# Second expert layer: token lists in place of cleared, scattered rows

## The chip, the cores and the metric

The kernel runs on one core of one Trainium2 chip. The metric is the device time of one launch in microseconds (us). A core has a matrix engine (TensorE, in the profile PE, with its weight loads as PEld), a vector engine (VectorE, DVE), an activation engine (ScalarE, ACT), a general engine (GpSimd, POOL) and a queue engine (SyncE, SP). They run side by side and wait for each other by semaphores. DMAs are issued by SP, ACT or POOL (queue entries are shown as SPq, ACTq, POOLq); one with row numbers in on-chip memory (gather, scatter, scatter-add) is issued by POOL and is shown as DMA_INDIRECT.

## The reference

Two transformer layers on x [4, 512, 256] (2048 tokens), each a cross attention on a context [4, 1601, 256] and a mixture-of-experts layer, all in fp32:

```python
x = x + xattn0(ctx, layernorm(x))      # 8 heads of 128; keys: 1601 context rows and 512 latents
x = x + moe0(layernorm(x))             # 8 experts, top 2, a capacity for each expert
x = x + xattn1(ctx, layernorm(x))      # 8 heads of 32, no bias
x = x + moe1(layernorm(x))             # 8 experts, top 2 by threshold, no capacity

def moe1(x):
    logits = x @ Wr + br
    thresh = second largest logit of each token
    weights = softmax(where(logits >= thresh, logits, -inf))
    h = gelu(x @ W1[e] + b1[e])                       # every expert e, 256 -> 1024
    return sum over e of weights[:, e] * (h @ W2[e] + b2[e])
```

Only two experts of a token have a weight, so the kernel sorts tokens by expert and computes tiles of 256 tokens of one expert.

## The kernel before, in words

The kernel has four stages, one after another on PE.

*First attention* (lines 528 to 898). A loop has 128 steps: 4 batches, 8 heads, 4 row tiles of 128. A step computes scores (L735, ten matmuls), their maximum (L743, DVE, `top`), the softmax (L749, ACT, into one of two `attn` buffers), then `exchange`: sixteen DMAs (L756) that swap 32-row blocks into `swapped`, twelve on SP's queue and four on ACT's. `turn` (L764, DVE) makes of it the transposed probabilities `pT`, which `weigh` (L772, PE) multiplies by the values a step or two later. Keys, values and the LayerNorm of the next batch's context (`ctx_b`) are spread over the steps as small pieces. Ahead of the loop, on SP, `clear_rows` (L370 to 380) fills two tables in HBM with empty rows, and `clear_slots` (POOL's queue) clears those of the first expert layer.

*First expert layer*, then *second attention*. During the second attention `route2` of the batch before runs in steps between other work: it normalises the rows of x (`pay`), finds each token's two experts, its weights and its place in the order of its expert, writes x with its weighted second bias to `out` (plain store), and scatters the rows (L521, POOL) into `rows_a` (2048 rows of 265 numbers: 256 of each expert, tokens of batches 0 to 2) or `rows_b` (18,688 rows: a place for every token and expert, all tokens). A row carries the normalised x, the token's number as a float, and its eight weights. Each of these scatters waits for the one before, since they write the same tensor. The framework orders instructions within each engine by what it knows of their readiness, so an engine's order isn't the order of the program text; the second attention has an order written out.

*Second expert layer* (lines 1375 to 1690). First 8 tiles, one for each expert, with the first 256 rows of `rows_a`; they need nothing of the last batch, whose routing runs between them (`routing`). Then 13 tiles (`SURE`) whose expert and first place come from a table worked out on the chip; further ones stand under a condition. In iteration k the loop does `hidden` of tile k (L1445, L1453), fetches tile k+2 (rows, and the expert's weights `w_e`, 2052 KB), makes tile k+1 `ready` (`turned`: transposes and a copy, L1433 and L1434; `told`: the token numbers `to`, L1395, and the weights `share`, L1423, L1594, L1595), and then `results` of tile k-1 (`second`, L1464; scaling into `y`, L1491; scatter-add into `out`, L1477, POOL). Rows have three buffers, `w_e` four, `to`, `share` and `y` five. Rows of the first 8 tiles come by plain SP loads, the later ones by POOL gathers (L1571; weights by L1583).

Of the kernel before, what the change touches and what calls it, by code (L numbers as in the profile page):

```python
# [8 lines left out]
F32 = mybir.dt.float32  # L9
I32 = mybir.dt.int32  # L10
# [6 lines left out]
P = 128  # L17
# [31 lines left out]

T = B * S  # L50
# [3 lines left out]
ROWS = E * PLACES  # L54
NG = (2 * T - 2 * G + E * (G - 1)) // G
SURE = 13
PAY = D + 1 + E
# [10 lines left out]
def xattn_ffn_twice(ctx: ExitStack, tc: tile.TileContext, a: dict, out: bass.AP):  # L68
# [107 lines left out]
    rows_a = dram.tile([E * G, PAY], F32, name="rows_a")  # L176
    rows_b = dram.tile([ROWS + G, PAY], F32, name="rows_b")
# [177 lines left out]
    taken_a = const.tile([P, E], F32, name="taken_a")  # L355

# [13 lines left out]
    def clear_rows(empty):  # L370

        nc.gpsimd.memset(empty, 0.0)
        nc.gpsimd.memset(empty[:, :, D : D + 1], NOWHERE)
        for rows in (rows_a, rows_b):
            n = rows.shape[0]
            for i in range(0, n, 4 * P):
                some = rows[i : min(i + 4 * P, n), :]
                nc.sync.dma_start(
                    some.rearrange("(p r) d -> p r d", p=P), empty[:, : some.shape[0] // P, :]
                )  # L380

    def route2(b, two, psum, tag, first=0, n=NT):
# [8 lines left out]
        for t in range(n):  # L391
            nc.vector.tensor_scalar(
                pay[:, t, :D],
                xb[:, t, :],
                mv[:, t, 0:1],
                rs[:, t : t + 1],
                ALU.subtract,
                ALU.mult,
            )
            nc.vector.tensor_scalar(  # L400
                pay[:, t, D : D + 1], lane, float((b * NT + first + t) * P), None, ALU.add
            )
# [39 lines left out]
        nc.vector.tensor_copy(pay[:, :, D + 1 :], wb)  # L442
# [74 lines left out]
        for rows, at in ((rows_a, place_a), (rows_b, place_b))[b == B - 1 :]:  # L517
            for k in range(2):
                for t in range(n):
                    j = b * NT + first + t  # L520
                    nc.gpsimd.indirect_dma_start(  # L521
                        out=rows[:, :],
                        out_offset=bass.IndirectOffsetOnAxis(ap=at[k][:, j : j + 1], axis=0),
                        in_=pay[:, t, :],
                        in_offset=None,
                        bounds_check=E * G - 1 if rows is rows_a else ROWS - 1,
                        oob_is_err=False,
                    )
                    yield


    with ExitStack() as st:
# [280 lines left out]
        empty = one.tile([P, 4, PAY], F32, tag="lat", name="empty")  # L813
        clear_rows(empty)
        clear_slots(empty[:, :, :D])
# [562 lines left out]
    with ExitStack() as st:  # L1378
# [8 lines left out]

        spare = st.enter_context(tc.tile_pool(name="d_spare", bufs=1))

        def told(rows, share_of):  # L1390

            to = five.tile([P, GR], I32, tag="to", name="to")
            share = five.tile([P, GR], F32, tag="share", name="share")
            for r in range(GR):
                nc.vector.tensor_copy(to[:, r : r + 1], rows[r][:, D : D + 1])  # L1395
                share_of(share[:, r : r + 1], rows[r][:, D + 1 :])
            return rows, to, share
# [4 lines left out]
        def first_tile(e):  # L1402

            rows = []
            for r in range(GR):
                got = three.tile([P, PAY], F32, tag=f"rows{r}", name=f"rows{r}")
                nc.sync.dma_start(got, rows_a[e * G + r * P : e * G + (r + 1) * P, :])
                rows.append(got)
            if e == 0:
                w2 = one.tile([P, WIDE - WB1], F32, name="w2_first")  # L1410
                nc.sync.dma_start(w2, a["wall"][:P, WB1:])
                w = lambda i, n: (
                    first_weights[i // D][:, i % D : i % D + n]
                    if i < WB1
                    else w2[:, i - WB1 : i - WB1 + n]
                )
            else:
                t = four.tile([P, WIDE], F32, tag="w", name="w_e")
                nc.sync.dma_start(t, a["wall"][e * P : (e + 1) * P, :])
                w = columns(t)  # L1420

            def share_of(to, weights):
                nc.vector.tensor_copy(to, weights[:, e : e + 1])  # L1423

            return w, rows, share_of
# [140 lines left out]
        def further_tile(i, three=three, four=four):  # L1566

            rows = []
            for r in range(GR):
                got = three.tile([P, PAY], F32, tag=f"rows{r}", name=f"rows{r}")  # L1570
                nc.gpsimd.indirect_dma_start(  # L1571
                    out=got,
                    out_offset=None,
                    in_=rows_b[:, :],
                    in_offset=bass.IndirectOffsetOnAxis(
                        ap=state["x_idx"][:, r, i : i + 1], axis=0
                    ),
                    bounds_check=ROWS + G - 1,
                    oob_is_err=False,
                )  # L1580
                rows.append(got)
            t = four.tile([P, WIDE], F32, tag="w", name="w_e")
            nc.gpsimd.indirect_dma_start(  # L1583
                out=t,
                out_offset=None,
                in_=a["wall"],
                in_offset=bass.IndirectOffsetOnAxis(ap=state["w_idx"][:, i : i + 1], axis=0),
                bounds_check=E * P - 1,
                oob_is_err=False,
            )  # L1590

            def share_of(to, weights):
                of = two.tile([P, E], F32, tag="told", name="told")
                nc.vector.tensor_tensor(of, weights, state["mine"][:, i, :], ALU.mult)  # L1594
                nc.vector.tensor_reduce(to, of, AX.X, ALU.add)  # L1595

            return columns(t), rows, share_of

# [5 lines left out]

        rest = routing()
        fetched = [first_tile(0), first_tile(1)]
        more = [lambda e=e: first_tile(e) for e in range(2, E)]
        more += [lambda i=i: further_tile(i) for i in range(SURE)]
        more.append(lambda: further_tile(SURE, spare, spare))

        def ready(w, rows, share_of):
            return (w, turned(rows), *told(rows, share_of)[1:])

        last = None
        next(rest)
        here = ready(*fetched.pop(0))
        for i in range(E + SURE):
            w, xT, to, share = here
            hT = hidden(w, xT)
            for _ in range(2):  # L1620
                next(rest, None)
            if more:
                fetched.append(more.pop(0)())
            if i + 1 < E + SURE:
                here = ready(*fetched.pop(0))
            next(rest, None)
            if last:
                results(*last)
            next(rest, None)
            last = (w, to, share, hT, T - S if i < E else T)  # L1630
# [4 lines left out]
        n_tiles = nc.values_load(state["counts"][0:1, 0:1], min_val=0, max_val=NG)  # L1635
        ties = nc.values_load(state["counts"][0:1, 1:2], min_val=0, max_val=E * T)

        def beyond(i, fetched=None):
            with tc.If(n_tiles > i):
                w, xT, to, share = ready(*(fetched or further_tile(i)))  # L1640
                results(w, to, share, hidden(w, xT))
                if i + 1 < NG:
                    beyond(i + 1)

        beyond(SURE, fetched.pop())
# [3 lines left out]
        with tc.If(ties > 0):  # L1649
            for b in range(B):  # L1650
                for t0 in range(0, NT, GR):
                    rows, acc = [], spare.tile([P, GR, D], F32, tag="acc", name="acc")
                    nc.vector.memset(acc, 0.0)
                    for r in range(GR):
                        j = b * NT + t0 + r
                        got = spare.tile([P, PAY], F32, tag=f"rows{r}", name=f"again{r}")
                        nc.vector.memset(got, 0.0)
                        for of, at in ((rows_a, place_a), (rows_b, place_b)):
                            nc.gpsimd.indirect_dma_start(
                                out=got,  # L1660
                                out_offset=None,
                                in_=of[:, :],
                                in_offset=bass.IndirectOffsetOnAxis(
                                    ap=at[0][:, j : j + 1], axis=0
                                ),
                                bounds_check=of.shape[0] - 1,
                                oob_is_err=False,
                            )
                        rows.append(got)
# [16 lines left out]
                    for r in range(GR):  # L1686
                        to = spare.tile([P, 1], I32, tag="to", name="to_t")
                        nc.vector.tensor_copy(to, rows[r][:, D : D + 1])
                        add_out(acc[:, r, :], to)
# [66 lines left out]
```

## Time and profile before

| | |
|---|---|
| Runs | 3011.76 to 3015.57 us, median 3014.13 (3 runs) |
| Profiled execution | 3014.63 us, its span 3012.6 us, mean granted PE clock 0.965 |
| PE busy | 2781.7 us (92% of the span), weight loads 1846.2 |
| DVE, ACT, POOL busy | 1444.5, 931.1, 473.7 us |
| Moved by DMA | 295.95 MB, mean 98 GB/s |
| Row scatters L521 | 24 into rows_a (32.1 us of POOL), 32 into rows_b (38.5) |
| Scatter-adds L1477 | 42, 66.4 us of POOL |

In a line of the timeline the columns are start, duration, engine, line, operation, output and inputs with shapes, count, and in brackets the idle time ahead and what ended it. A line of waits says which engine waited at which line for what: total us, times, longest. The page cuts the span into 40 equal slices; a digit is the busy share in tenths.

### The profile page before, as it was taken

What the parts mean: (1) busy time and instruction counts of PE and PEld (TensorE: products, weight loads), DVE (VectorE), ACT (ScalarE), POOL (GpSimd) and SP (SyncE); (2) the same over time, 40 slices, a digit from 0 to 9 for tenths busy, and PEclk for the clock granted to TensorE, in tenths of its full rate; (3) what the DMA queues carried; (4) which work ended last, traced back from release to release, by engine and by line L of the source; (5) the groups of instructions that cost most, each with busy time, mean ns of one, the idle gap of its engine ahead of it and who ended that gap; (6) DMA issues with size and microseconds to landing.
All of it is one profiled execution on the core that took longest, in us unless ns stands there. A gap on an engine that the chain in (4) does not pass through costs nothing. (4 is left out here: it accounts for less than half of the span.)

```text
span 3012.6 us, 35574 instructions
## 1 busy us (share of the span) xinstructions
PE 2781.7 (92%) x13426; PEld 1846.2 (61%) x13426; DVE 1444.5 (48%) x2324; ACT 931.1 (31%) x1312; POOL 473.7 (16%) x340
## 2 busy tenths in 40 slices
PE   5699999999999999999997999788988888898998
PEld 2466676666666667666665566544444444467887
DVE  4256447554476444464444100177775757751110
ACT  2233234232343333332321212123433434341221
POOL 1000000100001000010000100122424434343442
PEclk9899999999999999999998999889999999999999
DMA  8743334433343333333334233210101110045652
GB/s 297 234 123 94 99 92 105 112 96 92 94 113 104 98 86 95 93 102 97 92 96 148 93 98 105 66 27 14 30 26 36 30 35 22 13 172 165 193 171 73
DMA packets 165103, 295.95 MB, mean 98 GB/s; under 512 B 43287, under 2 KB 81752, under 8 KB 161848
## 3 DMA queue, kind: packets, MB, share of 16 engines
q1 hardware_dynamic: 124024, 204.45, 24.2%
q0 software_dynamic: 16320, 53.42, 5.9%
q10 hardware_dynamic: 24576, 35.68, 4.6%
q8 instruction: 109, 1.79, 0.3%
q14 instruction: 74, 0.61, 0.1%
HBM read 97.86 MB, written 49.76 MB: 49 GB/s over the span
## 5 line engine op out<-in xcount | busy, mean ns | idle before, releaser
L743 DVE TENSOR_REDUCE top<-ps_s 128x1 f32<-128x2113 f32 x128 | 301.8, 2358 | 578.9 <-PE ps_s L735 578.9
L772 PE MATMUL ps_o<-pT,v 128*128 128x256 f32 x2176 | 520.9, 381 | 7.8 <-DVE pT L764 7.8
L735 PE MATMUL ps_s<-kT,qT 128*128 128x512 f32 (+1 forms) x1280 | 489.0, 527 | 26.7 <-ACT attn L749 26.3
L772 PEld LDWEIGHTS ps_o<-pT,v 128*128 128x128 f32 x2176 | 410.9, 191 | 124.8 <-issue 69.9
L735 PEld LDWEIGHTS ps_s<-kT,qT 128*128 128x128 f32 x1280 | 241.5, 191 | 276.3 <-issue 239.9
L749 ACT ACTIVATE attn<-ps_s,top 128x2113 f32<-128x2113 f32 x128 | 258.9, 2023 | 486.1 <-DVE top L743 411.5
L764 DVE STREAM_TRANSPOSE pT<-swapped 128x2176 f32<-128x2176 f32 x128 | 312.4, 2441 | 70.2 <-DMA swapped<-attn 59.4
L1141 DVE TENSOR_REDUCE tops<-ps_s 128x2 f32<-128x800 f32 (+1 forms) x256 | 241.0, 984 | 150.7 <-PE ps_s L1133 150.6
L1180 PE MATMUL ps_w<-asked,keyed 64*128 64x256 f32 (+1 forms) x1664 | 243.7, 418 | 45.7 <-DVE tops L1141 39.4
L685 PE MATMUL ps_k<-kvin,wkv 128*128 128x512 f32 (+1 forms) x640 | 261.9, 533 | 5.2 <-ACT kT L692 5.2
L718 PE MATMUL ps_v<-wkv,kvin 128*128 128x256 f32 x1088 | 253.5, 381 | 0.0
L1202 POOL TENSOR_TENSOR sum<-sum,pT 128x1024 f32<-128x1024 f32 x80 | 197.0, 2463 | 334.4 <-ACT pT L1193 243.5
L1180 PEld LDWEIGHTS ps_w<-asked,keyed 64*128 64x128 f32 (+1 forms) x1664 | 150.4, 193 | 155.6 <-DVE tops L1141 79.7
L1193 ACT ACTIVATE pT<-ps_w 128x1024 f32<-128x1024 f32 (+1 forms) x176 | 178.2, 1023 | 195.4 <-PE ps_w L1180 191.8
L718 PEld LDWEIGHTS ps_v<-wkv,kvin 128*128 128x128 f32 x1088 | 204.9, 190 | 32.7 <-issue 3.4
L692 ACT ACTIVATE kT<-ps_k,bqk 128x512 f32<-128x512 f32 (+1 forms) x160 | 97.1, 620 | 268.1 <-DMA swapped<-attn 128.8
L685 PEld LDWEIGHTS ps_k<-kvin,wkv 128*128 128x128 f32 x640 | 116.5, 192 | 81.0 <-issue 67.1
L1202 DVE TENSOR_TENSOR sum<-sum,pT 128x1024 f32<-128x1024 f32 x96 | 153.3, 1597 | 6.2 <-ACT pT L1193 3.0
L725 ACT COPY v<-ps_v 128x512 f32<-128x512 f32 x144 | 79.8, 560 | 226.2 <-PE ps_v L718 154.0
L1445 PE MATMUL ps_h<-xT,w_e 128*128 128x256 f32 x640 | 143.7, 383 | 3.7 <-issue 3.7
L1133 PE MATMUL ps_s<-kT,qT 32*128 32x400 f32 (+1 forms) x1024 | 142.1, 582 | 3.2 <-ACT pT L1193 2.6
L1464 PE MATMUL ps_y<-w_e,hT 128*128 128x256 f32 x640 | 144.4, 385 | 0.0
(261 smaller groups left out, 2635.6 us busy)
## 6 DMA issues: line engine op xcount, KB each, us to landing
swapped<-attn SPq DMA_DIRECT2D x1536, 68.0 KB
swapped<-attn ACTq DMA_DIRECT2D x512, 68.0 KB
rows_b<-empty SPq DMA_DIRECT2D x36, 530.0 KB
w<-in_w_dram SPq DMA_DIRECT2D x16, 1024.0 KB
w_e<-in_wall_dram SPq DMA_DIRECT2D x7, 2052.0 KB
cT<-in_ctxT_dram SPq DMA_DIRECT2D x4, 1601.0 KB
keyed<-kT SPq DMA_DIRECT2D x32, 200.1 KB
ctx_b<-in_ctx_dram SPq DMA_DIRECT2D x4, 1536.0 KB
```

The source lines that it names most:

```text
L685: nc.tensor.matmul(ps[:, :n], lhsT=wkv[:, c, hs], rhs=flat_kvin[c][:, j0 : j0 + n], start=c == 0, stop=c == DC - 1,)
L718: nc.tensor.matmul(ps[:, k, :], lhsT=flat_kvin[c][:, j * P : (j + 1) * P], rhs=wkv[:, c, cols], start=c == 0, stop=c == DC - 1,)
L735: nc.tensor.matmul(flat[:, j0 : j0 + n], lhsT=qT[:, t * P : (t + 1) * P], rhs=kT[:, j0 : j0 + n], start=True, stop=True,)
L743: nc.vector.tensor_reduce(top, flat[:, :L], AX.X, ALU.max, negate=True)
L749: nc.scalar.activation(attn[:, :L], flat[:, :L], AF.Exp, bias=top, accum_out=total)
L764: nc.vector.transpose(pT[:, :, k * P : (k + 1) * P].rearrange("p c (a i) -> p a c i", a=4), swapped.rearrange("p a (c i) -> p a c i", i=32),)
L772: nc.tensor.matmul(ps, lhsT=v[:, j - parts[part][0], (h % 2) * DH0 : (h % 2 + 1) * DH0], rhs=pT[:, j, :], start=j == 0, stop=j == NB - 1,)
L1141: nc.vector.tensor_reduce(tops[u][:, t, 2 * pair : 2 * pair + 2, k], pss[pair][:, :, : hi - lo], AX.X, ALU.max,)
L1180: nc.tensor.matmul(ps[:r, s, pair * QH : (pair + 1) * QH], lhsT=keyed[o][64 * s : 64 * s + 64, pair, j * P : j * P + r], rhs=asked[u % 3][ ...
L1193: nc.scalar.activation(pT[:r], ps[:r], AF.Exp)
L1202: (nc.gpsimd if k else nc.vector).tensor_tensor(to, to, pT[:r], ALU.add)
L1464: nc.tensor.matmul(ps, lhsT=hT[:, f, r * P : (r + 1) * P], rhs=w(WB1 + f * D, D), start=f == 0, stop=f == FC - 1,)
```

## The change

The rows of the second expert layer are no longer scattered by expert. Each batch's `pay` (256 + 8 numbers a row, the token number gone) is stored in token order by a plain SP DMA into `rows_a` (1537 rows) and `rows_b` (2049 rows; both for batches 0 to 2), the last row being zeros. What is scattered by expert and place is the token's number alone, 4 bytes, into `list_a` (2048) and `list_b` (18,688), which are filled with a number that stands for no token by one small DMA each. A tile loads its list one tile ahead of its rows (`listed`: an SP load for the first 8 tiles, two POOL gathers for later ones), and gathers its rows by it (`fetched`: two POOL gathers, for the first 8 tiles too). The list is also the address of the scatter-adds (`to`, now in seven buffers), so the casts of L1395 and the lane addition in `route2` fall away. The branch for ties reads rows in order; it isn't entered here.

```diff
-PAY = D + 1 + E
+PAY = D + E
...
-    rows_a = dram.tile([E * G, PAY], F32, name="rows_a")
-    rows_b = dram.tile([ROWS + G, PAY], F32, name="rows_b")
+    list_a = dram.tile([E * G, 1], I32, name="list_a")
+    list_b = dram.tile([LIST + G, 1], I32, name="list_b")
+    rows_a = dram.tile([TA + 1, PAY], F32, name="rows_a")
+    rows_b = dram.tile([T + 1, PAY], F32, name="rows_b")
...
-        for rows in (rows_a, rows_b):
-            n = rows.shape[0]
-            for i in range(0, n, 4 * P):
-                some = rows[i : min(i + 4 * P, n), :]
-                nc.sync.dma_start(
-                    some.rearrange("(p r) d -> p r d", p=P), empty[:, : some.shape[0] // P, :]
-                )
+    def clear_lists(zeros, nobody):
+        for rows, of, n in ((rows_a, list_a, TA), (rows_b, list_b, T)):
+            per = of.shape[0] // P
+            nc.gpsimd.memset(nobody[:, :per], n)
+            nc.sync.dma_start(of.rearrange("(p r) o -> p (r o)", p=P), nobody[:, :per])
+            nc.sync.dma_start(rows[n : n + 1, :], zeros)
...
-            nc.vector.tensor_scalar(
-                pay[:, t, D : D + 1], lane, float((b * NT + first + t) * P), None, ALU.add
-            )
...
+            nc.sync.dma_start(
+                rows[at0 : at0 + n * P, :].rearrange("(t p) d -> p t d", p=P), pay
+            )
             for k in range(2):
                 for t in range(n):
                     j = b * NT + first + t
                     nc.gpsimd.indirect_dma_start(
-                        out=rows[:, :],
+                        out=of[:, :],
                         out_offset=bass.IndirectOffsetOnAxis(ap=at[k][:, j : j + 1], axis=0),
-                        in_=pay[:, t, :],
+                        in_=token[:, j : j + 1],
...
+        seven = st.enter_context(tc.tile_pool(name="d_seven", bufs=7))
...
-                nc.vector.tensor_copy(to[:, r : r + 1], rows[r][:, D : D + 1])
...
+        def listed(k, pool):
+            to = pool.tile([P, GR], I32, tag="to", name="to")
+            if k < E:
+                of = list_a[k * G : (k + 1) * G, :].rearrange("(p r) o -> p (r o)", p=P)
+                nc.sync.dma_start(to, of)
+                return to
+            for r in range(GR):
+                nc.gpsimd.indirect_dma_start(
+                    out=to[:, r : r + 1],
+                    out_offset=None,
+                    in_=list_b[:, :],
+                    in_offset=bass.IndirectOffsetOnAxis(
+                        ap=state["x_idx"][:, r, k - E : k - E + 1], axis=0
+                    ),
...
+        def fetched(k, to, three=three, four=four):
+            of, n = (rows_a, TA) if k < E else (rows_b, T)
             rows = []
             for r in range(GR):
                 got = three.tile([P, PAY], F32, tag=f"rows{r}", name=f"rows{r}")
-                nc.sync.dma_start(got, rows_a[e * G + r * P : e * G + (r + 1) * P, :])
+                nc.gpsimd.indirect_dma_start(
+                    out=got,
+                    out_offset=None,
+                    in_=of[:, :],
+                    in_offset=bass.IndirectOffsetOnAxis(ap=to[:, r : r + 1], axis=0),
...
+        lists = [listed(k, seven) for k in range(3)]
+        tiles = [fetched(k, lists[k]) for k in range(2)]
...
-            if more:
-                fetched.append(more.pop(0)())
+            if k + 2 <= n_tiles:
+                pools = (three, four) if k + 2 < n_tiles else (spare, spare)
+                tiles.append(fetched(k + 2, lists[k + 2], *pools))
+            if k + 3 <= n_tiles:
+                lists.append(listed(k + 3, seven if k + 3 < n_tiles else spare))
```

## The prediction

> **What bounds the kernel now.** I read first the forty slices of the page, to find where TensorE (PE) is not the bound:
>
> ```profile
> PE   5699999999999999999997999788988888898998
> PEclk9899999999999999999998999889999999999999
> DMA  8743334433343333333334233210101110045652
> ...
> rows_b<-empty SPq DMA_DIRECT2D x36, 530.0 KB
> ```
>
> A slice is 75.3 us. PE is at 90% or more nearly everywhere; only the first two slices fall short while DMA is at its fullest, and the clearing of `rows_b` stands there. The table by stretch (columns: PE, its weight loads, DVE, ACT, POOL; clock, DMA share, GB/s) and PE's waits from 45 to 150 us show it closer:
>
> ```profile
> 40.00:100.00 60.00, 52.26 (x168) 30.26 (x167) 11.03 (x13) 19.03 (x30) 5.18 (x8) 0.94 1.02 380
> 100.00:110.00 10.00, 0.00 (x0) 0.00 (x0) 0.00 (x0) 0.00 (x0) 0.00 (x0) 0.72 0.87 308
> 110.00:150.00 40.00, 26.50 (x79) 16.16 (x80) 18.45 (x13) 8.66 (x10) 0.00 (x0) 0.81 0.48 115
> ...
> PE ps_s L735 <- ACT attn L749: 24.3, 3, 18.7
> PE ps_k L685 <- ACT kT L692: 5.2, 1, 5.2
> ```
>
> The DMA engines are full from 40 to 100 us, all engines stand still at 100 to 110, and PE waits 29.5 us in all. From 150 to 1500 us PE waits 0.2 us. The timeline names the chain:
>
> ```profile
> 39.18 62.92 SPq L378 DMA_DIRECT2D rows_b<-empty  x37
> 59.47 2.02 ACT L749 ACTIVATE attn<-ps_s,top 128x2113 f32<-128x2113 f32 x1 [4.79 <-DVE top L743]
> 77.15 3.77 PE L735 MATMUL ps_s<-kT,qT 128*128 128x512 f32 x10
> 102.20 33.25 SPq L756 DMA_DIRECT2D swapped<-attn  x42
> 115.61 2.44 DVE L764 STREAM_TRANSPOSE pT<-swapped 128x2176 f32<-128x2176 f32 x1 [32.30 <-DMA swapped<-attn]
> 117.82 5.63 PE L735 MATMUL ps_s<-kT,qT 128*128 128x512 f32 x10 [18.66 <-ACT attn L749]
> ```
>
> The first softmax is done at 61.5 us, but the 12 of its 16 exchange DMAs that go through SP's queue stand behind 37 clears until 102.2; its turn comes at 115.6. In steady state the same step takes 10 us (softmax ended 141.84, turn 151.75).
>
> The second place is the start of the last loop (tiles of the second expert layer), in DVE's and PE's waits from 2670 to 2760 us and the timeline:
>
> ```profile
> DVE to L1395 <- DMA out_dram<-y,to: 32.5, 2, 16.8
> ...
> PE ps_x L1504 <- DVE xT L1434: 8.1, 1, 8.1
> ...
> 2702.10 0.97 POOL L521 DMA_INDIRECT rows_b<-pay,place_b  x1 [2.05 <-DMA rows_b<-pay,place_b]
> 2710.01 0.97 POOL L521 DMA_INDIRECT rows_b<-pay,place_b  x1 [6.95 <-DMA rows_b<-pay,place_b]
> 2721.37 8.83 PE L1445 MATMUL ps_h<-xT,w_e 128*128 128x256 f32 x32 [2.98 <-issue]
> 2749.44 7.07 PE L1445 MATMUL ps_h<-xT,w_e 128*128 128x256 f32 x32
> ...
> 2829.38 1.05 POOL L1571 DMA_INDIRECT rows<-rows_b,x_idx  x1 [2.72 <-PE tp L1433]
> 2832.34 0.17 DVE L1594 TENSOR_TENSOR told<-rows,mine 128x8 f32<-128x8 f32 x1 [0.45 <-DMA rows<-rows_b,x_idx]
> ```
>
> Tiles 0 to 4 begin at 2674.59, 2688.5, 2703.98, 2721.37, 2749.44: 74.9 us for four, where later ones take 14.25 each (57.0): 17.9 us are lost. The reason: the `to` cast needs a buffer whose scatter-add is late, because POOL's last eight row scatters wait for one another. From tile 7 on PE is the bound, exactly 14.25 us a tile.
>
> **What the Trainium skill says.** (1) "DMA: Bandwidth & Descriptors", section "Issuing engines are not separate DMA queues": all issuers share the 16 engines. The trace agrees: share 1.02 while SP's queue clears, and the four exchange DMAs on ACT's queue are slow too. (2) Same page, "Queues, rings and completion order": an engine takes turns between queues by packets. So a scatter of small rows crawls beside a big load; the trace shows it as 2702.10 to 2710.01 under a weight load, where 2699.08 to 2702.10 was free: +5 us. (3) Same page, "Anatomy of one DMA", about 2.0 us fixed: the gather issued at 2829.38 for 1.05 us was used at 2832.34, about 1.9 us after its issue. (4) "TensorE: Matmul & The Clock Gate", Part 1: an idle PE loses clock. Ten score matmuls took 5.63 us at 117.82 and 3.77 at 77.15, clock 0.72 in between.
>
> **The change, part by part.**
>
> *Clears.* Removed: 41 SP DMAs of about 530 KB (21.5 MB, at 380 GB/s by that 57 us of all engines). Added: four small ones. The exchange then follows the softmax by 10 us. But as built, the batch-1 context load goes up ahead of the first exchange on SP (its buffer is free about 43.3; 1.5 MB, landing about 53), and on DVE the statistics of that context, some 8 us of work, stand ahead of the first `top`. So I put the first top at 61.5 (was 57.1), softmax end 66, turn 76.5. PE's own work ahead of the fourth tile's scores ended at 117.8 - 18.7 = 99.2; in the built order 16.1 us of it stand behind these scores, so it ends at 83.1, and the third softmax, which waits for the first exchange, can be done by 76.5 + 2.2 = 78.7. So the wait of 18.7 goes, but for 1.3 that I give for the later first tops: 17.4. The other waits, 24.3 - 18.7 + 5.2 = 10.8, are partly the pipeline filling up again, which some of it does in any case; I take half, 5.4. Sum -22.8, taken -23; bounds -16 (statistics later still, or exchange beside the slot clears and weight loads) and -29 (all of the idle time). The DVE work is only moved: DVE is busy 48% of the span, so its old place stays empty at no gain; ahead of the first top it costs the 4.4 us counted above, at most its 8.
>
> *First attention to second attention.* The middle keeps its engine orders. Seven SP stores of `pay` (540 KB each) come in beside the store of x: 7 x 0.4 us of SP, landing where DMA is at 0.0 to 0.4. The list scatters are as many as the row scatters (24 + 32), 1.0 us of POOL each as before. Sixteen lane adds and 42 casts of 0.15 us leave DVE, about 8 us in all, not on the path. An iota of 0.17 comes in. Taken: 0; bounds -2 to +2. The cover is SP's and DVE's idle time beside a busy PE; if it were gone, the 7 issues would cost 2.8 us.
>
> *Start of the last loop.* Before, rows of tiles 0 to 2 were loaded by SP at 2649. Now SP must load lists into buffers whose memory the second attention holds to its end (POOL's last sum ends 2671.55, the last `got` about 2675.0), so lists land about 2677; then POOL gathers, two per tile at 1.03 us. As built, DVE copies shares of tiles 0 and the first of tile 1 before `xT` of tile 0, so three gathers must land: 2677 + 3 x 1.03 + 2 + 0.14 + 0.68 gives about 2683.7, +9. But three weight loads (6.2 MB, 16 us) are issued by SP just behind the lists and fill the engines to about 2693; by (2) each gather then costs +5 or ends with the loads: 2692 to 2696, +17 to +22. I take +17, the lower end, since a gather can land before the last of the loads. Further, shares of tiles 4 and 5 stand on DVE ahead of `xT` of tiles 2 and 3, and their gathers on POOL behind list scatters that wait for routing: new waits of 0 to 10, taken 5. Waiting behind them on DVE: x additions and `xT`, so PE. The old loss of 17.9 goes nearly whole, since `to` comes by DMA into seven buffers: -17. What is late next is the gather behind the list scatters, the 5 above. Sum 17 + 5 - 17 = +5; bounds -8 and +15.
>
> *Tiles 7 to 20.* POOL per tile: 2 x 1.03 + 1.04 + 2 x 1.59 = 6.3 us, now two list gathers more: 8.3 of 14.25. List gathers stand behind the weight gather, so they land slowly (up to 8 us), but are needed a tile later. Behind them on POOL stand the scatter-adds, waited for only through five buffers. Taken 0; if that cover is gone, up to 2.1 us x 13 = 27.
>
> Sum on the profiled execution (3014.63; span 3012.6 and 2.0 around it): 3014.6 - 23 + 0 + 5 = 2996.6. The median shown is 0.5 lower: 2996.
>
> **Rivals.**
>
> *A, the start of the loop isn't crowded* (chance 0.18): gathers slip in between weight packets (+9), no new waits: 9 - 17 = -8; 3014.6 - 23 - 8 = 2983.6. For: only 3 x 128 rows over 16 engines, 24 each. Against: the +5 us at 2702.10.
>
> *B, the front's gain is mostly eaten* (0.14): the statistics ahead of the first top, waiting for a load behind others, leave 16; the loop costs 10 more: 3014.6 - 16 + 10 = 3008.6. For: DMA still has slot clears and weights in the first 60 us. Against: 21.5 of its MB go.
>
> *C, slower: POOL paces the last loop* (0.10). A list gather under a weight load, then row gathers that wait for it in POOL's order, hold scatter-adds and the next weight gather. It decides once POOL's waits in a tile go over 14.25 - 8.3 = 5.9 us; one gather under load waits 5 + 2 = 7. At 2 to 3 us a tile, 13 x 2.5 = 32: 3014.6 - 23 + 5 + 32 = 3028.6. Against: the wait comes a tile later than the issue.
>
> *D, the change doesn't do what it says* (0.03): some other load takes the queue's place before the first exchange: 3014.
>
> **How the numbers follow.** The likeliest case has 0.55 (2988 to 3004). About 0.2%, or 6 us, is what a measurement can tell from no change: under 3008.1 is faster. Faster: 0.55 + 0.18 + 0.06 of B = 0.79; same: 0.08 of B + 0.03 of D = 0.11; slower 0.10 of C. The range 2978 to 3012 leaves out C, D, 0.03 of B and 0.03 below: 0.19. By the bounds of the parts alone it would be 3014.1 - 29 - 2 - 8 = 2975 to 3014.1 - 16 + 2 + 15 = 3015; the ends don't come together.
>
> **What would show it.** Front: no clear of rows, first turn near 76, PE's waits from 45 to 150 us under 10 instead of 29.5, no 10 us of standstill. Loop: first tile near 2692 - 23 = 2669 of the new clock; no wait of `to` on `out_dram`; waits of `share` on gathers among tiles 2 to 5; tiles 7 to 20 at 14.25. The prediction is wrong if the first turn comes after 90, if the steady tile is over 14.25, or if the first tile starts within 10 us of the second attention's end.

## The result, and the profile after

The changed kernel takes 3031.56 us (median of 4 runs, 3025.88 to 3034.86) against 3013.01 us of the kernel before on the same chip: a ratio of 1.0058, 95% interval 1.0044 to 1.0072. It is 18.5 us slower. The forecast was faster, 2996 us, in a range of 2978 to 3012.

The profiled execution of the changed kernel took 3025.88 us, the fastest of its four runs; its span is 3024.1 us. What follows explains the 11.5 us between the two profiled spans. The other three runs took 3 to 9 us more, at a mean granted clock of 0.960 to 0.963 against 0.964 here. There is no trace of them, and where their time lies isn't known.

The start of the same piece of work in both traces:

| Place in the kernel | before, us | after, us | after minus before |
|---|---|---|---|
| 2% of the score matmuls of both attentions (early in the first) | 136.30 | 111.22 | -25.1 |
| 30% of them (about the middle of the first) | 913.06 | 889.62 | -23.4 |
| first expert layer begins | 1709.72 | 1686.43 | -23.3 |
| second attention, last `ps_w` matmul | 2664.76 | 2637.94 | -26.8 |
| POOL's last `sum` of the second attention ends | 2671.55 | 2651.78 | -19.8 |
| tile 0 begins | 2674.59 | 2675.15 | +0.6 |
| tile 4 begins | 2749.44 | 2753.72 | +4.3 |
| tile 7 begins | 2793.20 | 2802.12 | +8.9 |
| tile 20 begins | 2978.49 | 2987.40 | +8.9 |
| end of the span | 3012.58 | 3024.07 | +11.5 |

So the front gave what was forecast, and the start of the last loop took back all of it and 11.5 us more. The PE and DMA rows of the changed kernel's page, its stretches, and PE's waits of the front (45 to 150 us):

```profile
PE   4999999999999999999996999688989887868997
DMA  6333443434434433344333322200110101045652
```

```profile
40.00:100.00 60.00, 49.30 (x148) 27.03 (x149) 37.31 (x99) 24.64 (x36) 7.09 (x12) 0.91 0.46 136
100.00:110.00 10.00, 10.00 (x45) 8.24 (x44) 2.96 (x3) 4.16 (x6) 0.00 (x0) 1.00 0.37 93
110.00:150.00 40.00, 40.00 (x142) 25.61 (x141) 19.71 (x17) 12.03 (x15) 0.00 (x0) 1.00 0.39 93
```

```profile
PE ps_k L688 <- DVE qT L680: 6.3, 1, 6.3
PE ps_s L738 <- ACT attn L752: 2.7, 2, 2.0
```

From 40 to 100 us the DMA share fell from 1.02 to 0.46, the standstill at 100 to 110 us became ten busy microseconds, and PE waits 9.3 us (with 0.3 for `kT`) where it waited 29.8. The granted clock from 100 to 150 us is 1.00, where it was 0.72 and 0.81. The loop's start is the other way round. PE's waits and DVE's waits of the changed kernel from 2630 to 2800 us:

```profile
PE tp L1475 <- DMA rows<-rows_a,to: 17.0, 2, 15.5
PE ps_n L1235 <- POOL sum L1207: 9.5, 1, 9.5
PE ps_y L1506 <- DVE y L1533: 5.1, 2, 2.9
PE ps_h L1487 <- issue: 5.1, 1, 5.1
PE tp L1475 <- DVE share L1461: 4.4, 1, 4.4
```

```profile
DVE share L1461 <- DMA rows<-rows_a,to: 39.7, 6, 13.3
DVE told L1464 <- DMA rows<-rows_b,to: 30.4, 4, 14.7
```

The wait of the `to` cast for `out_dram` is gone, as forecast. But PE waits 17 us for gathered rows, 9.5 us for POOL's last sum, and DVE 39.7 us for gathers with `share` copies at the head of its order. The timeline (POOL, and in the last line PE) shows what neither the forecast nor its rivals had:

```profile
2641.80 0.99 POOL L524 DMA_INDIRECT list_b<-token,place_b  x1 [1.26 <-DVE sum L1207]
2642.81 2.36 POOL L1207 TENSOR_TENSOR sum<-sum,pT 128x1024 f32<-128x1024 f32 x1
2648.42 0.99 POOL L524 DMA_INDIRECT list_b<-token,place_b  x1 [3.25 <-DMA list_b<-token,place_b]
2649.42 2.37 POOL L1207 TENSOR_TENSOR sum<-sum,pT 128x1024 f32<-128x1024 f32 x1
2653.54 0.99 POOL L524 DMA_INDIRECT list_b<-token,place_b  x1 [1.76 <-DMA list_b<-token,place_b]
2661.82 1.04 POOL L1425 DMA_INDIRECT rows<-rows_a,to  x1 [1.15 <-issue]
2670.17 0.48 PE L1475 MATMUL tp<-ident,rows 128*128 128x128 f32 x1 [15.47 <-DMA rows<-rows_a,to]
```

The scatter of up to 128 numbers of 4 bytes that was issued at 2648.42 took 4.9 us to land, and POOL's next scatter, at 2653.54, stood still for it; a `sum` in order behind such a scatter waits as well. Counted from the landings in the trace, a `list_b` scatter takes 4.7 us from issue to landing in the third batch (median of eight, issued 2621.6 to 2659.7) and 5.9 us in the last batch (eight, 2695.1 to 2735.9). Other traffic isn't the reason for the first: from 2601.4 to 2637.9 us the DMA share was 0.02, and three scatters that began and landed there took 4.1 to 4.5 us.

### The profile page after: what moved, and what is told of

Read it like the earlier page. It is cut to its first block, busy times and chain, and to the rows that moved or that the text cites. A ratio compares the mean times of both kernels' runs of the same rounds, so it can differ in the third digit from the quotient of the medians.

```text
span 3024.1 us, 35562 instructions
## 1 busy us (share of the span) xinstructions
PE 2779.2 (92%) x13426; PEld 1846.8 (61%) x13426; DVE 1438.3 (48%) x2266; ACT 931.9 (31%) x1312; POOL 515.6 (17%) x386
## 3 DMA queue, kind: packets, MB, share of 16 engines
q1 hardware_dynamic: 120956, 184.17, 22.8%
## 5 line engine op out<-in xcount | busy, mean ns | idle before, releaser
L775 PEld LDWEIGHTS ps_o<-pT,v 128*128 128x128 f32 x2176 | 410.8, 191 | 125.2 <-issue 70.3
```

Source lines behind the costliest of these rows:

```text
L775: nc.tensor.matmul(ps, lhsT=v[:, j - parts[part][0], (h % 2) * DH0 : (h % 2 + 1) * DH0], rhs=pT[:, j, :], start=j == 0, stop=j == NB - 1,)
```

## The experiments

All times are medians beside runs of the kernel before on the same chip. Differences between experiments are taken from the profiled spans where parts of a span are meant.

**The front: what about the clears costs it?**

Clears on POOL's queue:

```diff
-                nc.sync.dma_start(
-                    some.rearrange("(p r) d -> p r d", p=P), empty[:, : some.shape[0] // P, :]
-                )
+                pieces.append(
+                    lambda some=some: nc.gpsimd.dma_start(
+                        some.rearrange("(p r) d -> p r d", p=P),
+                        empty[:, : some.shape[0] // P, :],
+                    )
+                )
...
+        for k, f in enumerate(clears):
+            later[4 + k // 2].append(f)
```

In the program text the clears now stand among the loop's steps; in the trace POOL issues them from 45.3 to 110.1 us, behind the slot clears.

> The kernel before, with its 41 clears of rows issued by POOL instead of SP, behind the slot clears; nothing else changed. If what cost the front was the order of SP's queue (twelve exchange DMAs behind 37 clears), the first turn comes soon after the first softmax although the DMA engines stay full, and most of the front's 23 us come back: about 2995, between 2990 and 3002. If it was the bandwidth that the clears take, the exchange only shares it, and no more than 10 us come back: 3004 to 3014.

Measured: 3028.23 us, ratio 1.0045 (1.0031 to 1.0060): no gain, a loss of 14 us. The kernel's stretches show the engines still full, now for longer:

```profile
40.00:100.00 60.00, 39.36 (x104) 18.61 (x102) 21.91 (x72) 17.20 (x25) 24.66 (x44) 0.80 0.99 370
100.00:110.00 10.00, 0.90 (x2) 0.81 (x3) 1.78 (x1) 0.85 (x2) 3.10 (x7) 0.64 1.01 345
```

The exchange is issued at once behind its softmax (80.96 us) and its turn comes at 108.22, 27 us later, where an undisturbed one takes 10. Taking the order of SP's queue away gains nothing as long as the DMA engines are full. The first softmax itself is late too, at 78.8 us. On DVE the statistics of the next batch's context, which ran after it in the kernel before, stand ahead of the first `top` here, and they waited 20.6 us for the load of that context, which runs beside the clears:

```profile
69.00 0.75 DVE L120 BATCH_NORM_STATS2 st<-ctx_b 128x6 f32<-128x256 f32 x2 [20.63 <-DMA ctx_b<-in_ctx_dram]
```

Clears in the first expert layer, six for each expert, with a source tile of their own there and one small POOL instruction that ties them to their place:

```diff
-        clear_rows(empty)
...
+            nc.gpsimd.tensor_scalar(
+                nothing[:, 0, 0:1], sxT[:, 0, 0:1], 0.0, None, ALU.mult
+            )
+            for f in clears[e * 6 : (e + 1) * 6]:
+                f()
             hT = expert(ps_h, two, sxT, w1, gelu_tanh)
```

> The kernel before with its 41 clears moved into the first expert layer, six for each expert, still issued by SP; lists and rows as before. Theory (the clears cost the front because they fill the DMA engines while the first exchange runs, not for being there): the front runs as in the changed kernel, the first expert layer hides 21.5 MB in 350 us, the last loop is that of the kernel before; 2985 to 2995. Rival (the clears are paid wherever they stand, here by late loads of rows or weights in the first expert layer): 3005 or more.

Measured: 2992.57 us, ratio 0.9933 (0.9913 to 0.9952). The same clears cost nothing there: over 320 us of that layer (1690 to 2010 us; 1710 to 2030 in the kernel before) PE is busy 291.76 us against 291.90, while the DMA share rises from 0.26 to 0.43. So it is the bytes at the time of the first exchange that cost the front. Its gain is shown by itself, without any list: -20.5 us at the last `ps_w` matmul, and tiles 0 to 4 take 75.1 us as before (74.9).

**The loop: does a scatter of 4-byte entries set the pace?**

Entries of 64 bytes, the number written sixteen times:

```diff
+WD = 16
...
-    list_a = dram.tile([E * G, 1], I32, name="list_a")
-    list_b = dram.tile([LIST + G, 1], I32, name="list_b")
+    list_a = dram.tile([E * G, WD], I32, name="list_a")
+    list_b = dram.tile([LIST + G, WD], I32, name="list_b")
...
-                        in_=token[:, j : j + 1],
+                        in_=token[:, j, :],
```

> The changed kernel, with list entries of 64 bytes (the token's number sixteen times) instead of 4. Rival (scatters of 4 bytes to neighbouring places land late, 4 to 5 us against 2.8 for whole rows, and their chain holds POOL's last sum and the gathers behind it): a list scatter lands after 2 to 3 us, POOL's last sum ends 5 to 7 us sooner, the whole 7 to 12 us faster, about 3021. Theory (memory and the chained list and gather): the sum sooner by some us at most, the whole 0 to 7 us faster, 3024 to 3031.

Measured: 3007.04 us, ratio 0.9981 (0.9971 to 0.9990), 24 us less than the changed kernel and more than either theory gave. A `list_b` scatter lands after 2.3 us in the third batch and 2.2 us in the last (medians of eight). POOL's last sum ends 7.4 us after the last `ps_w` matmul instead of 13.8, and tiles 0 to 4 take 63.7 us instead of 78.6. POOL's waits for one scatter before the next from 2560 to 2800 us, of the kernel before, of the changed kernel and of this one:

```profile
POOL rows_b L521 <- DMA rows_b<-pay,place_b: 26.0, 8, 6.9
```

```profile
POOL list_b L524 <- DMA list_b<-token,place_b: 27.5, 8, 6.0
```

```profile
POOL list_b L525 <- DMA list_b<-token,place_b: 8.4, 6, 3.2
```

The change did not make the total of these waits much longer (27.5 us against 26.0). What is new is what stands behind them on POOL: the gathers of the first eight tiles' rows, which SP loaded before.

Is it the size of the write, or that neighbouring entries are written at once? Entries of 4 bytes, 64 bytes apart, in the second list alone:

```diff
-    list_b = dram.tile([LIST + G, 1], I32, name="list_b")
+    list_b = dram.tile([(LIST + G) * WD, 1], I32, name="list_b")
...
+                nc.vector.tensor_scalar(at, at, float(WD), None, ALU.mult)
                 nc.vector.tensor_copy(place_b[k][:, mine_b], at)
```

> The changed kernel with 4-byte entries of the second list put 64 bytes apart (indices times sixteen, the list sixteen times as long and cleared whole); the scatter still writes 4 bytes, the first list is as it was. Theory N (the scatters land late because neighbouring entries, written by different DMA engines, share a stretch of memory): the second list's scatters land after 2 to 3 us as with 64-byte entries, 3005 to 3013. Theory S (a write of 4 bytes is slow by its size): they still land after 4.5 to 6 us, 3025 or more.

Measured: 3010.62 us, ratio 0.9990 (0.9982 to 0.9998). The scatters still write 4 bytes each and land after 2.4 us in both batches. The size of the write is not the cause; the nearness of the entries is. The first list of this kernel, left at 4 bytes side by side, agrees: its scatters of the first batch land after 5.5 us (median of eight), against 3.0 us in the kernel with 64-byte entries in both lists. POOL's waits and two lines of its timeline:

```profile
POOL list_b L531 <- DMA list_b<-token,place_b: 10.5, 7, 3.2
...
2636.33 0.99 POOL L531 DMA_INDIRECT list_b<-token,place_b  x1 [0.15 <-issue]
2639.88 0.99 POOL L531 DMA_INDIRECT list_b<-token,place_b  x1 [0.17 <-issue]
```

Scatters 3.5 us apart no longer wait for each other. Entries of 16 bytes, side by side (the edit of the 64-byte kernel with `WD = 4`):

> The changed kernel with list entries of 16 bytes, side by side. Theory N: four entries share what sixteen shared before, so the scatters land between the two, 2.5 to 4 us, 3007 to 3020. Theory S: by size alone, anything between the 4-byte and the 64-byte kernel; the two theories part in the run with spaced entries, and this one shows how wide an entry must be.

Measured: 3009.16 us, ratio 0.9985 (0.9978 to 0.9992), landings of 2.3 and 2.2 us. Entries of 16 bytes side by side land as fast as those of 64; widths between 4 and 16 bytes were not tried.

**The loop: the lists' memory, and list and gather in a chain**

```diff
-        seven = st.enter_context(tc.tile_pool(name="d_seven", bufs=7))
...
+    seven = ctx.enter_context(tc.tile_pool(name="d_seven", bufs=7))
     gat = ctx.enter_context(tc.tile_pool(name="gat", bufs=2 * NT))
```

> The changed kernel, with the list buffers in a pool that is opened after the first attention and stays open, so that their memory is free while the second attention runs. Theory (the wait of the lists for the second attention's memory, then list and gather one behind the other under the weight loads, costs some 20 us ahead of the first tile): the lists load when the last list scatter has landed, the first two tiles' rows come before the end of the second attention, the first tile starts 12 to 20 us sooner; 3012 to 3018 against 3031. Rival (slow 4-byte scatters set the pace): the first tile starts at most 5 us sooner, 3026 or more.

Measured: 3030.10 us, ratio 1.0051 (1.0035 to 1.0068): no gain, as the rival had it, but for another reason. Tile 0 begins 3.0 us after POOL's last sum instead of 23.4, so the 20 us between them were the chain. But the last `ps_w` matmul comes 7.6 us later, the sum a further 3.6, and tiles 0 to 4 take 93.4 us instead of 78.6. The six gathers of the first three tiles now stand on POOL from 2632 to 2641 us, ahead of the last five sums, and PE waits 4.2 us for a `pT` there. With the slow scatters cured the same was tried again: 64-byte entries and early lists for tiles 0 to 2,

```diff
+            if k < 3:
+                to = to3[:, k]
+                of = list_a[k * G : (k + 1) * G, 0:1].rearrange("(p r) o -> p r o", p=P)
+                nc.sync.dma_start(to, of)
+                return to
```

> The changed kernel with 64-byte entries and with the lists of tiles 0 to 2 in memory that is free before the second attention ends. Theory (two costs that hide each other: each of them alone leaves the other late): the first tile starts within 5 us of POOL's last sum instead of 21, 12 to 18 us sooner than with wide entries alone; 2989 to 2995. Rival (the gathers that go early push POOL's sums and scatters back by as much): 3002 to 3008, as with wide entries alone.

Measured: 3008.62 us, ratio 0.9986 (0.9978 to 0.9994), the same as wide entries alone. The rival held, though the time lies just above its range: tile 0 begins 10.7 us sooner, tile 4 at 2735.50 against 2735.39. And 16-byte entries with all seven list buffers early (the two edits together):

> The changed kernel with 16-byte entries and all list buffers (seven) in memory that is free before the second attention ends. If what gives back the early start with wide entries and three early lists is that the fourth list still waits for the second attention's memory, the gain stays: 2994 to 3002 against 3009 with 16-byte entries alone. If it is the gathers of tiles 3 to 5 under the weight loads, with DVE's share copies ahead of the routing, the first tile starts 10 us sooner and tile 4 no sooner: 3004 to 3010.

Measured: 3004.35 us, ratio 0.9965 (0.9951 to 0.9979), about 5 us less than 16-byte entries alone. Tile 0 begins 10.4 us sooner, tile 4 by 4.7. Of the two cases it is nearer the second. Its timeline:

```profile
2661.82 1.28 SPq L1449 DMA_DIRECT2D w_e<-in_wall_dram  x3
2663.60 1.05 POOL L1429 DMA_INDIRECT rows<-rows_a,to  x1 [2.69 <-DVE rs L140]
2670.68 0.15 DVE L1465 COPY share<-rows 128x1 f32<-128x1 f32 x1 [6.49 <-DMA rows<-rows_a,to]
2676.39 0.69 DVE L110 COPY xnT<-tp 128x512 f32<-128x512 f32 x1 [3.51 <-PE tp L164]
```

Three weight loads go out, a gather of tile 3 behind them lands 7 us after its issue (2663.60 to 2670.68), DVE waits for it 6.5 us with a `share` copy, and the routing of the last batch, which tile 1 and the list scatters follow, stands behind that copy. Also, the six early gathers stand ahead of POOL's sums: the last one ends 14.8 us after the last `ps_w` matmul, against 7.4.

**Half of the change**

First tiles' rows scattered and loaded as before, lists for the later tiles alone:

```diff
+                if k < E:
+                    nc.sync.dma_start(got, rows_a[k * G + r * P : k * G + (r + 1) * P, :])
+                else:
+                    nc.gpsimd.indirect_dma_start(
...
+                if first:
+                    nc.vector.tensor_copy(to[:, r : r + 1], rows[r][:, D : D + 1])
```

> Half of the change: the first eight tiles' rows are scattered by expert and loaded by SP as in the kernel before (their table, 2 MB, cleared by four SP DMAs, casts of the token number kept), and only the later tiles use token-ordered rows and a list. Theory (the start of the last loop loses it all): the first tile starts within 8 us of the second attention's last weighing, as before, the front's gain is kept; 2986 to 2996. Rival (POOL's list gathers pace the later tiles): 3000 or more, with tiles 8 to 20 over 14.25 us each.

Measured: 3028.18 us, ratio 1.0039 (1.0024 to 1.0054). My theory at that point (the chain of list and gather loses it all) fell here: tile 0 does begin 3.0 us after POOL's last sum, and yet nothing is won. The sum ends 15.8 us after the last `ps_w` matmul and tiles 0 to 4 take 87.6 us: the 4-byte scatters. Tiles 8 to 20 take 14.25 us each, so the rival's mechanism was wrong too. With 64-byte entries in this kernel's list:

> The half change (first eight tiles' rows as before, lists for the later ones) with 64-byte entries in its list. Theory (late scatters of 4 bytes held POOL's last sum and the first tiles, and the chain of list and gather costs 20 us of its own): the sum ends about 5 us after the last weighing instead of 16, the first tile starts 3 us later, tiles 0 to 4 take no more than the 75 us of the kernel before; 2985 to 2995. Rival (the first tiles stay held by the eight serial scatters of the last batch whatever their width): 3000 to 3010.

Measured: 2995.84 us, ratio 0.9943 (0.9924 to 0.9962), 32 us less than with 4-byte entries. Sum 6.7 us after the matmul, tiles 0 to 4 in 66.8 us. POOL's waits from 2560 to 2800 us, of the half change with 4 and with 64 bytes:

```profile
POOL list_b L528 <- DMA list_b<-token,place_b: 47.4, 12, 6.9
```

```profile
POOL list_b L529 <- DMA list_b<-token,place_b: 17.0, 9, 3.6
```

Eight buffers instead of five for the cast token numbers, in this kernel and in the kernel before with its clears moved:

```diff
-            to = five.tile([P, GR], I32, tag="to", name="to")
+            to = eight.tile([P, GR], I32, tag="to", name="to")
```

> The half change with 64-byte entries, and eight buffers instead of five for the token numbers that are cast for the first eight tiles. Theory (between tiles 3 and 4 a cast waits for the scatter-add that still reads its buffer): the step from tile 3 to tile 4 falls from 22.7 to 14 to 16 us, 2986 to 2990. Rival (the next wait takes its place, tile 8's gathers on DVE ahead of the copies): 2992 to 2996.

> The kernel before with the clears in the first expert layer, and eight buffers instead of five for the token numbers. Theory (the 17.9 us that tiles 0 to 4 lost before are waits of the cast for scatter-adds, as the prediction had it): tiles 0 to 4 take 60 to 64 us instead of 75, 2972 to 2980. Rival (the serial row scatters hold y or x additions as well, and the wait moves there): 2984 to 2992.

Measured: 2991.40 us, ratio 0.9931 (0.9912 to 0.9950), and 2984.86 us, ratio 0.9909 (0.9890 to 0.9928). In the first, the step from tile 3 to tile 4 falls from 22.7 to 14.9 us, but 4.7 us come back at tiles 4 to 7, and the two intervals (0.9943 and 0.9931) overlap. In the second, tiles 0 to 4 take 58.4 us instead of 75.1, all but 1.4 us of what was lost there; tiles 4 to 7 then take 52.8 instead of 44.2. Its four runs (2983.7 to 2985.7 us) all lie below the four with five buffers (2990.6 to 2995.6). So both sides of its expectation hold in part. PE's and DVE's longest waits of that kernel from 2640 to 2790 us:

```profile
PE ps_y L1478 <- DVE y L1505: 7.5, 1, 7.5
...
DVE to L1409 <- DMA rows<-rows_b,x_idx: 43.1, 7, 20.0
```

The next to be late is the cast of tile 8's numbers, which stands on DVE ahead of `y` and waits for the first gather from `rows_b`. This last kernel is the fastest of all that were tried: the old scatter of whole rows, no lists, the clears where DMA engines are idle, and three more small buffers.

## Why the prediction was wrong, point by point

- *The clears.* Forecast -23, measured -23.4 at 30% of the score matmuls. The size was right, in part by luck. PE's waits shrank by 20.5 us, less than the 22.8 of the sum. The rest fits the clock, which the forecast named and left out of its sum: up to the 2% mark of the table PE was busy 76.2 us before and 70.3 after, at mean clocks of 0.90 and 0.95. The reason was half right: that the exchange DMAs "stand behind 37 clears until 102.2" named SP's order, and with the clears on another queue the loss stayed (3028.23). By the Trainium skill (DMA: Bandwidth & Descriptors, "Issuing engines are not separate DMA queues") DMAs run on the same 16 DMA engines whichever engine issues them; the trace agrees, with a share of 0.99 from 40 to 100 us for the clears on POOL's queue and 1.02 on SP's. The first turn came at 82.1 us, forecast near 76. (The cleared tables are 20,736 rows of 1060 bytes, which is 22.0 MB and not 21.5.)
- *First attention to second attention.* This is the first step that failed: "The list scatters are as many as the row scatters (24 + 32), 1.0 us of POOL each as before", taken at 0. Issue did stay at 1.0 us; the landing didn't. The forecast priced a scatter by POOL's busy time, though it had itself read that each waits for the landing of the one before. In the third batch whole rows landed 3.0 us after issue (median of eight in the trace of before), 4-byte entries 4.7 us; in the last batch the entries took 5.9. Curing that alone took 24 us off the changed kernel and 32 us off the half change. The second attention itself ended 3.4 us sooner still. The lists are not the likely reason: between a quarter and a half of its `ps_w` matmuls the changed kernel took 184.2 us and the kernel before 188.7, with the same waits of PE, but the granted clock was 1.00 from 2226 to 2312 us where it was 0.93 and 0.96 in the same work before.
- *Start of the last loop, first tile.* Forecast +17, measured 37.2 us from the last `ps_w` matmul to tile 0 instead of 9.8: +27.4. Seven of these are POOL's sum behind slow scatters (13.8 instead of 6.8 us). The other 20.3 are the chain of list and gather under the weight loads, which was forecast at 17; its mechanism was right (rows issued 2661.82, used 2670.17). (2677 and the terms behind it add up to 2682.9 and not 2683.7, so rival A's +9 should be +8; the +17 does not rest on it.)
- *New waits +5 and old loss -17.* Forecast -12 for tiles 0 to 4, measured +3.7 (78.6 against 74.9). The old loss was sized rightly: eight buffers alone removed 16.7 us in the kernel before. But the waits that took its place were 20 us and not 5, above all gathers queued on POOL among slow list scatters (27.5 us of waits) and copied by DVE ahead of everything else. With 64-byte entries the same span is 63.7 us, 11.1 below before, close to the forecast -12.
- *Tiles 7 to 20.* Forecast 0, and exactly 14.25 us each: rival C's mechanism (POOL pacing the loop) was wrong, and that its 3028.6 us came near the 3031.56 measured is luck. Tiles 4 to 7 lost 4.6 us: in the trace the list gathers of tiles 8 to 10 wait on POOL for scatter-adds ahead of them (8.6 us in two waits), and DVE for tile 8's rows. From the start of tile 20 to the end it took 2.6 us more; after the last scatter-add 11.0 us go by instead of 8.6. Neither loss was tried by itself.

The sum in the profiled pair: -26.8 + 27.4 + 3.7 + 4.6 + 2.6 = +11.5. With 64-byte entries, whose scatters land even sooner than whole rows, the kernel still takes 3007 us and not 2996. Its profiled span against that of before shows why: -21.8 us up to the last `ps_w` matmul (forecast -23), +18.9 from there to tile 0 (+17), -11.1 for tiles 0 to 4 (-12), but +5.4 for tiles 4 to 7 and +2.3 from tile 20 on, both taken at 0. So once the landing is cured, each priced term holds within 2 us, and most of what is still missing lies in the two stretches that had no term.

## What to carry to other kernels

When DMAs wait for each other, price them from issue to landing, not by their issuing engine's busy time, and look for that number in the trace whenever the size or the place of the data changes. Before work is removed because it stands in the way, try it in a stage where its resource is idle: moving the clears kept 20.5 us of the gain with none of the new waits. A copy that an in-order engine runs early, because its data were expected early, makes everything behind it wait for a transfer.

## What the runs showed of the hardware

A scatter of up to 128 entries of 4 bytes into a list whose entries lie side by side landed 4.7 to 5.9 us after its issue (medians of the third and the last batch); with the same 4-byte writes 64 bytes apart it took 2.4 us, with 16-byte and with 64-byte entries side by side 2.2 to 2.3. The small write costs nothing by itself here, and crowding does. Why crowding costs, no run shows.

It also goes with how many entries are written. In `route2` a place below 256 of an expert's order goes to the first list and a later one to the second, and each scatter passes over what is outside its list (`bounds_check`), so the first list should fill in the early batches and the second in the later ones. In the changed kernel the scatters into the first list landed after 5.6, 3.5 and 2.5 us (medians, batch by batch), those into the second after 2.9, 3.7, 4.7 and 5.9. How many entries each scatter wrote isn't on record.
